# A graph layer's edge rows picked from three bfloat16 parts instead of float32 halves

## The chip, the core and the metric

The kernel runs on one core of one Trainium2 chip. Five engines of the core matter here: PE multiplies matrices (its weight loads are listed apart as PEld), DVE does elementwise work and reductions, ACT does copies and activation functions, POOL issues the indirect transfers that scatter rows, and SP issues most of the other transfers. Each engine works through its own instructions in the order of the program and stops at an instruction whose inputs aren't there. The metric is the device time of one execution in microseconds. Before the change it was 2373.37 us (median of 3 runs, 2369.18 to 2377.8).

## The reference

There are 12500 nodes with 64 features and 212500 edges (`src`, `dst`), sorted by `dst`, each with a weight. Each edge's input is put together from its two nodes and its weight and goes through two layers; the results are summed by `src`, and two more layers give the node's new features.

```python
h = jnp.maximum(_layernorm(x, axis=-1), 0.0)
edge_in = jnp.concatenate([h[src], h[dst], edge_weight1], axis=1)
e = silu(edge_in @ eW1 + eb1)
e = silu(e @ eW2 + eb2)
agg = segment_sum(e, src, num_segments=12500)
node_in = jnp.concatenate([h, agg], axis=1)
out = x + silu(node_in @ nW1 + nb1) @ nW2 + nb2
```

## The kernel before

The first layer is split by its inputs. For every node two rows of 128 numbers are worked out once: table `ta` (the part that comes from the `src` node) and table `tb` (from the `dst` node; `tb0` is a copy of the part that the first edges need). What an edge needs is then `ta[src] + tb[dst] + weight * eW1[last] + eb1`.

**Sending (`send_all`, `count`, `send`).** The edges are taken in 208 blocks of 1024, two blocks to a pair. As edges are sorted by `dst`, the 256 edges of a quarter of a block find all their `tb` rows in a window of 30 rows. `windows` loads the eight windows of a pair into one of three `win` buffers; a quarter's window lies on 32 partitions, on rows 30 and 31 of which stand `eW1[last]` and `eb1`. `load_rows` brings the edges' row numbers within their windows (`bc`, repeated on 32 partitions) and `count` compares them on DVE with the partition's number (L408, or L406 and L402 for the last and first pairs): `pick` has a one where an edge's row is. `weights` loads the edge weights into row 30 of each quarter of `pick`, and row 31 is one. `send` multiplies `pick` by `win` on PE in float32, on 64 partitions at a time (L475), which gives `tb[dst] + weight * eW1[last] + eb1` for 2 x 128 edges; ACT copies it to a buffer `qs` and writes the edge's place within its bucket beside it (L484, L485); POOL scatters 128 rows by one indirect transfer to the list `q` in DRAM (L488). The rows are sorted into 100 buckets of 125 `src` nodes: where a row goes is worked out in `count`, from how many of each bucket came before (L393 to L451), and is handed to POOL in the tile `to` (4 buffers). There are 16 buffers of `qs`, each with two tiles of 128 edges.

**Steps.** The rows of the buckets are read back in 18 levels of 25 batches, 450 steps in all (`s_lr` to `s_add`), each with 4 tiles of 128 edges: PE builds one-hot matrices, adds `ta[src]` (L596, L610, L616), ACT applies Silu (L620), PE the second layer (L648), ACT Silu again (L652), PE sums by node (L662), DVE adds to `aggT` (L673). The load of a batch (`fetch`, L559, on SP) waits until the scatters of all blocks of its level have landed. In the last level the node part (`nodes`) follows.

**Order.** The order of the instructions on PE, DVE, ACT and SP is written out by hand. Ahead of the steps stands the start: `first_rows` makes the four groups of `tb0`, `destinations` and `by_edges`, `sources` and `scale` turn the edge lists into bucket numbers, `products` makes 25 groups each of `ta` and `tb`, while the first blocks are already sent. A list of generators (`feed`) deals out the pieces of this between the pieces of `send_all`. Later, `marks` says how many pieces of sending are to stand before each step, and they are put between the stages of the steps. POOL's own order is that in which the scatters are written.

Of the kernel before, what the change touches and what calls it, by code (L numbers as in the profile page):

```python
# [42 lines left out]
SPAN = 7 * STEP + WL  # L43
# [21 lines left out]
FILL0, FILL_EACH, FILL_LATE = 18, 2, 8  # L65
AFTER = mybir.DependencyInfo(mybir.DependencyClass.Sync, mybir.DependencyReason.DATA)
# [8 lines left out]
def tile_gnn(ctx: ExitStack, tc: tile.TileContext, x, src, dst, ew, eW1, eb1, eW2, eb2, nW1, nb1, nW2, nb2, out):  # L75
# [105 lines left out]
    for g in range(2):  # L181
        nc.vector.tensor_scalar(
            same0[:, g : g + 1], plus, float(STEP), float(g * NQR * STEP), op0=OP.mult, op1=OP.add
        )
    nc.vector.tensor_scalar(plus, same, float(WL + 1), None, op0=OP.is_equal)
# [15 lines left out]
    tb = dram.tile([P * NB, H], F32, name="tb")  # L201
    dests = dram.tile([NP, NQR, 2, QR], BF16, name="dests")

    tb0 = dram.tile([FRONT + P * NE, H], F32, name="tb0")
    ta_buckets, tb_buckets = (t.rearrange("(l b) f -> l b f", b=NB) for t in (ta, tb))

    def product(s, hr, ps, tag, to):

        abs_ = []
        for a in range(2):  # L210

            half = slice(a * D, (a + 1) * D)
            ab = ps.tile([P, G // 2, H], F32, name="ab", tag=tag)
            for i in range(G // 2):
                nc.tensor.matmul(ab[:, i], hr[half, i, :], w1[half, s, :], start=True, stop=True)  # L215
            abs_.append(ab)
        for a in range(2):
            nc.scalar.copy(to.rearrange("l (i a) h -> l a i h", a=2)[:, a], abs_[a])
# [12 lines left out]
    wins = [const.tile([P, 2, 2, H], F32, name=f"win{i}") for i in range(NW)]  # L231
    nc.vector.memset(wins[0], 0.0)

    def extra_rows(dma, wins):

        for win in wins:
# [69 lines left out]
    qsp = ctx.enter_context(tc.tile_pool(name="qs", bufs=16))  # L306
    top = ctx.enter_context(tc.tile_pool(name="to", bufs=4))
    with ExitStack() as work:
# [17 lines left out]
        def load_rows(s):  # L326

            if s < nblocks:
                p, g = s // 2, s % 2
                if p == 0:  # L330
                    lists[p] = [None, None]
                    blk[s] = [None]
                    return
                if g == 0:
                    bc = ld.tile([P, 2, QR], BF16, name="bc")
                    lists[p] = [bc, None]
                    r = dests[p, 0, 0]
                    of = bass.AP(tensor=r.tensor, offset=r.offset, ap=[[2 * QR, NQR], [0, 32], [1, 2 * QR]])
                    nc.sync.dma_start(bc.rearrange("p g e -> p (g e)"), of)
                blk[s] = [lists[p][0][:, g]]  # L340

        def windows(p):

            table, front, end = (tb, FRONT, NB * P) if 2 * p >= EARLY else (tb0, 0, NE * P)
            if p == 0:
                table, end = tb0[: FRONT + G * P], G * P
            assert 2 * p < EARLY or len(done_b) == NB // G
            at = nc.sync.value_load(base_i[:, p : p + 1], min_val=front, max_val=FRONT + end - SPAN)
            for a in range(NQR):
# [3 lines left out]
                nc.sync.dma_start(wins[p % NW][a * 32 : a * 32 + WL, :, a % 2, :], of)  # L353

        def load(s):

            if s < nblocks:
                p, g = s // 2, s % 2
                if g == 0:
                    if p != 1:  # L360
                        windows(p)
                    lists[p][1] = ld.tile([P, 2, QR], F32, name="pick")
                blk[s] += [wins[p % NW][:, g], lists[p][1][:, g]]
            if s:
                load_rows(s + 1)

        def weights(s):

            if s < nblocks:
                p, g = s // 2, s % 2  # L370
                pick = lists[p][1][:, g]
                e0 = s * BLK
                m = 1 if e0 + 2 * BLK > E else 2
                if m == 2 or e0 + BLK <= E:
                    of = bass.AP(tensor=ew.tensor, offset=ew.offset + e0, ap=[[QR, NQR], [BLK, m], [1, QR]])
                    nc.sync.dma_start(lists[p][1][WL::32, g : g + m, :], of)
                else:
                    for a in range(NQR):
                        m = min(QR, E - e0 - a * QR)
                        if m > 0:  # L380
                            of = bass.AP(tensor=ew.tensor, offset=ew.offset + e0 + a * QR, ap=[[m, 1], [1, m]])
                            nc.sync.dma_start(pick[a * 32 + WL : a * 32 + WL + 1, :m], of)

        def count(s):

            if s < nblocks:
                bc, win, pick = blk[s]
                p, g = s // 2, s % 2
                whole = p > 0 and (2 * p + 2) * BLK <= E
# [15 lines left out]
                elif not whole:  # L405
                    nc.vector.tensor_scalar(pick, bc, same, plus, op0=OP.is_equal, op1=OP.add)  # L406
                elif g == 0:
                    nc.vector.tensor_scalar(lists[p][1], lists[p][0], same, plus, op0=OP.is_equal, op1=OP.add)  # L408
            yield
            if s < nblocks and p and (g == 0 or not whole):  # L410
                weights(s)
# [45 lines left out]
        def send(s):  # L457
# [6 lines left out]
            places = locE[:, g * TB : (g + 1) * TB, p].rearrange("p (i a t) -> p i t a", a=2, i=2)  # L464
            for t, i in itertools.product(range(2), range(2)):
                if i or t:
                    yield
                if i == 0:
# [9 lines left out]
                tiles = [j for j in (4 * i + t, 4 * i + 2 + t) if j < nt]  # L478
# [3 lines left out]
                qp = qps[i]  # L482
# [235 lines left out]
        def first_rows(g):  # L718

            hr = turned(x0, g)  # L720
            yield
            got = fp.tile([P, G, H], F32, name="got")
            product(1, hr, mm, "mm", got)
            yield
            nc.scalar.dma_start(tb0[FRONT + g * P : FRONT + (g + G) * P, :].rearrange("(p j) f -> p j f", j=G), got)
# [12 lines left out]
        def products(b0, g, xs):  # L738
# [15 lines left out]
            product(1, hr, mm, "mm", got)  # L754
            yield
            nc.sync.dma_start(tb_buckets[:, b : b + G, :], got)
# [15 lines left out]
        def destinations():  # L772
# [21 lines left out]
            for g in range(2):  # L794
                nc.vector.tensor_tensor(
                    rowsD[:, :, g, :],
# [98 lines left out]

        def checks():
# [24 lines left out]
        done_a, done_b, ready, scaled = [], [], set(), set()  # L921
# [12 lines left out]
        with tc.tile_pool(name="lists", bufs=1, side="right") as lp:  # L934
            x0 = lp.tile([P, NE, D], F32, name="x0")
            plus0 = lp.tile([P, 2, QR], F32, name="plus0")
            pair0 = lp.tile([2 * NQR, 2, P], F32, name="pair0")
# [12 lines left out]
            nc.sync.dma_start(tb0[:FRONT], zeros[:FRONT, :H])  # L950
            extra_rows(nc.sync.dma_start, wins[:1])
# [3 lines left out]
            f, sf = (lp.tile([NP, PAIR], F32, name=n) for n in ("f", "sf"))  # L955
# [6 lines left out]
            rowsD = lp.tile([NP, NQR, 2, QR], BF16, name="rowsD")  # L962
# [28 lines left out]
            list(table)  # L991
# [10 lines left out]
            list(counting)  # L1002
            todo = groups()
# [7 lines left out]
            for win in wins[1:]:  # L1011
                nc.vector.memset(win, 0.0)
            extra_rows(nc.sync.dma_start, wins[1:])
# [11 lines left out]
            lists_on = itertools.chain(*(g for part_ in parts for g in (sources(*part_), scale(*part_))), checks())  # L1025
# [96 lines left out]
def general_sums(tc, N, E, NB, H, src, dst, ew, ta, tb, aggT, w1d, eb1b, w2, ident, ones, eb2r, part):  # L1122
# [6 lines left out]
    with ExitStack() as ctx:  # L1129
# [17 lines left out]
        def tile_of(at, n):  # L1147
# [10 lines left out]
            for k, (idx, table) in enumerate(((si, ta[:]), (di, tb[:]))):  # L1158
                got = gw.tile([P, H], F32, name=f"got{k}")
# [6 lines left out]
                nc.vector.tensor_tensor(pre[:n], pre[:n], got[:n], op=OP.add)  # L1166
# [76 lines left out]
```

## Time and profile before

| | |
|---|---|
| median of 3 runs | 2373.37 us |
| profiled execution | 2374.24 us |
| its span | 2372.4 us |
| granted PE clock, mean | 0.962 |
| busy: PE, DVE, POOL, ACT | 89%, 78%, 72%, 50% |

The span goes from the first instruction of the profiled execution to its last. The page cuts it into 40 slices of 59 us and gives each engine's busy share in tenths. A group's row has the line, engine, operation, what it writes and reads, how often; then its busy time in us and the mean length of one in ns; then how long the engine stood idle just before instructions of the group, and which work ended most of that idle time. Names of tiles have their buffer numbers left out. POOL's indirect transfers are counted as busy while it writes their descriptors, not until the data have landed. Line numbers are those of the kernel before.

### The profile page before, as it was taken

The numbers are of one execution on the slowest core, as the hardware profiler recorded it, in microseconds if no ns is written. First come the engines' busy times: TensorE is split into PE (matmuls) and PEld (weight loads), VectorE is DVE, ScalarE is ACT, GpSimd is POOL, SyncE is SP. The second block draws the span as 40 slices with busy tenths as digits, with TensorE's granted clock in tenths as the row PEclk, the third lists the DMA queues.
The fourth block names the chain that finished last, engine by engine and source line by source line (L and its number), as shares of the span: only waits on it lengthen the run. The fifth ranks groups of instructions, "written<-read, shape, count | busy, mean of one in ns | idle before, by whom it ended". The sixth has DMA issues, their size and how long they took to land.

```text
span 2372.4 us, 49836 instructions
## 1 busy us (share of the span) xinstructions
PE 2103.3 (89%) x17399; PEld 1847.2 (78%) x17399; DVE 1857.0 (78%) x3291; ACT 1180.9 (50%) x3262; POOL 1697.3 (72%) x1711
## 2 busy tenths in 40 slices
PE   3685888789999999998999889999989999999998
PEld 2452667678888888887788778888878888889998
DVE  7985667678888888787888788878788888788665
ACT  3463554445555555554445445545455555555543
POOL 5677777777777777777777777777777777777310
PEclk9975899899999999999999999999999999999999
DMA  4475676555555555555555555555654444444564
GB/s 136 156 251 194 218 242 190 166 185 174 178 180 173 170 177 176 173 170 157 170 164 172 168 162 172 164 167 170 190 165 131 134 135 135 137 135 141 160 214 122
DMA packets 241429, 401.83 MB, mean 169 GB/s; under 512 B 47528, under 2 KB 140195, under 8 KB 240965
## 3 DMA queue, kind: packets, MB, share of 16 engines
q1 hardware_dynamic: 149411, 216.21, 30.7%
q0 software_dynamic: 53568, 123.20, 14.5%
q10 hardware_dynamic: 38192, 59.17, 8.8%
q8 instruction: 139, 2.28, 0.4%
q14 instruction: 119, 0.97, 0.1%
HBM read 191.09 MB, written 207.01 MB: 168 GB/s over the span
## 4 chain that ended last, share of the span: by engine, by line
PE 50%; DMA 22%; DVE 11%; POOL 6%; issue 6%; ACT 4%; DVEq 0%; SPq 0%; ACTq 0%; POOLq 0%
DMA q<-qs,to 16%; PE seg L662 11%; PE pt L616 10%; PE p L648 8%; POOL q L488 6%; PE qp L475 6%; DMA qt<-q 6%; PE pt L610 6%; PE lr L596 3%; DVE aggT L673 2%; DVE each L398 1%; PE ab L215 1%; ACT e L620 1%; PE z L286 1%; PE o L295 1%
## 5 line engine op out<-in xcount | busy, mean ns | idle before, releaser
L488 POOL DMA_INDIRECT q<-qs,to x1661 | 1669.2, 1005 | 542.5 <-issue 306.1
L620 ACT ACTIVATE e<-pt 128x512 f32<-128x512 f32 x450 | 268.9, 597 | 765.5 <-PE pt L616 704.3
L662 PE MATMUL seg<-one,e 128*128 128x125 f32 x3600 | 505.0, 284 | 106.1 <-DVE aggT L673 89.4
L662 PEld LDWEIGHTS seg<-one,e 128*128 128x128 f32 x3600 | 445.9, 195 | 144.3 <-DVE aggT L673 72.8
L648 PE MATMUL p<-w,e 128*128 128x128 f32 x3600 | 486.1, 278 | 0.0
L648 PEld LDWEIGHTS p<-w,e 128*128 128x128 f32 x3600 | 441.9, 192 | 12.5 <-issue 10.5
L484 ACT COPY qs<-qp 128x256 f32<-128x256 f32 x831 | 309.2, 372 | 266.6 <-PE qp L475 261.4
L601 DVE TENSOR_SCALAR oneT<-lr,part 125x512 f32<-125x512 f32 x450 | 335.1, 745 | 19.2 <-PE lr L596 12.8
L673 DVE TENSOR_TENSOR aggT<-aggT,seg 128x500 f32<-128x500 f32 x425 | 284.4, 669 | 64.6 <-PE seg L662 61.2
L475 PE MATMUL qp<-win,pick 64*128 64x256 f32 x1662 | 319.3, 452 | 17.0 <-ACT qs L484 5.9
L629 DVE TENSOR_TENSOR one<-nodes,qt 128x500 f32<-128x500 f32 x450 | 302.7, 673 | 0.0
L610 PE MATMUL pt<-ident,qt 128*128 128x128 f32 x1800 | 286.1, 283 | 1.4 <-ACT zn L267 0.9
L652 ACT ACTIVATE e<-p 128x512 f32<-128x512 f32 x450 | 269.6, 599 | 30.2 <-PE p L648 18.9
L642 ACT COPY p<-b2f 128x512 f32<-128x512 f32 x450 | 267.6, 595 | 0.0
L616 PE MATMUL pt<-oneT,al 125*128 125x128 f32 x1952 | 262.2, 278 | 0.0
L451 DVE SCALAR_TENSOR_TENSOR to<-rank,offE 128x8 int32<-128x8 f32 x208 | 36.6, 176 | 286.7 <-DMA q<-qs,to 282.1
L616 PEld LDWEIGHTS pt<-oneT,al 125*128 125x128 f32 x1952 | 242.2, 195 | 0.0
L447 DVE TENSOR_TENSOR mine<-oh,counts 128x800 f32<-128x800 bf16 x208 | 204.0, 981 | 39.8 <-PE counts L432 39.5
L596 PE MATMUL lr<-identb,qt 128*125 128x128 bf16 x1800 | 186.9, 228 | 49.6 <-DMA qt<-q 49.1
L610 PEld LDWEIGHTS pt<-ident,qt 128*128 128x128 f32 x1800 | 196.5, 145 | 27.2 <-issue 22.9
L596 PEld LDWEIGHTS <-qt 128*125 128x125 bf16 x1800 | 156.9, 141 | 76.3 <-DMA qt<-q 63.7
L449 DVE TENSOR_REDUCE rank<-mine 128x8 f32<-128x800 f32 x208 | 205.1, 986 | 7.2
(176 smaller groups left out, 1945.7 us busy)
## 6 DMA issues: line engine op xcount, KB each, us to landing
qt<-q SPq DMA_DIRECT2D x450, 288.0 KB
q<-zeros ACTq DMA_DIRECT2D x70, 720.0 KB
q<-qs,to POOLq DMA_INDIRECT x1661
bc<-dests SPq DMA_DIRECT2D x103, 128.0 KB
win<-tb SPq DMA_DIRECT2D x416, 30.0 KB
tb<-got SPq DMA_DIRECT2D x25, 256.0 KB
zd<-zn SPq DMA_DIRECT2D x25, 250.0 KB
zh<-zd SPq DMA_DIRECT2D x25, 250.0 KB
```

The source lines that it names most:

```text
L475: nc.tensor.matmul(qps[i_][:, :m], pick[half, t * P : (t + 1) * P], win[half, :m], start=True, stop=True)
L484: nc.scalar.copy(qs[:, :m, :H], qp[:, :m, :])
L488: ins = nc.gpsimd.indirect_dma_start(out=q[:], out_offset=bass.IndirectOffsetOnAxis(ap=to[:k, j : j + 1], axis=0), in_=qs[:k, a, :], in_of ...
L596: nc.tensor.matmul(lr[:L, t, :], loc[:, at : at + 1].to_broadcast([P, L]), identb, start=True, stop=True)
L601: nc.vector.tensor_scalar(oneT, st[k].pop("lr")[:L], part1[:L, :], None, op0=OP.is_equal)
L610: nc.tensor.matmul(pt[:, t, :], qt[:, j, :H], ident, is_transpose=True, start=t == 0, stop=False, skip_group_check=True)
L616: nc.tensor.matmul(pt[:, cols, :], a[:L, b, :], oneT[:, cols, :], start=False, stop=True, skip_group_check=True)
L620: nc.scalar.activation(e1, pt, AF.Silu)
L629: nc.vector.tensor_tensor(one.rearrange("p (b j) l -> p b j l", j=n), nodes1[:, None, None, :].to_broadcast(wide), loc[:, tiles[0][1] : ti ...
L648: nc.tensor.matmul(p2[:, t, :], e1[:, t, :], w2, start=False, stop=t == G - 1, skip_group_check=True)
L662: nc.tensor.matmul(item[2][:, b, :], e2[:, t, :], one[:, t, :], start=j < G, stop=j >= G * (n - 1))
L673: nc.vector.tensor_tensor(v, v, seg, op=OP.add)
```

## The change

The rows of `tb` are kept as three bfloat16 parts, which together hold the float32 value, side by side in DRAM. A window then takes 32 rows of three parts each, that is 96 partitions, and 12 more partitions take `eW1[last]` and `eb1` in their parts against the parts of the edge weights and ones: 108 partitions (`K3`) in all. All eight windows of a pair are brought by one load, the row numbers of all 2048 edges by one (`picks`, repeated on 96 partitions) and the weights' parts by one. The compare is done in place on 96 x 2048 bfloat16, once for a pair. `send` has one bfloat16 product of 108 partitions for every 128 edges, where one float32 product on 64 partitions served 256 edges. The first pair is still done in float32, from a table `tbF` of its own.

What must be worked out for this: `product` splits each group of `tb` into three parts (two copies, two subtractions, one copy, one subtraction, through `got3`, which has one buffer), `split` does the same to the first group, `first_weights` to the weights of the first pairs and to the two extra rows, and `other_weights` to the rest of the weights, in eight pieces, dealt out at the head of the lists. The edge lists are turned to float32 in place, and `qs` has 10 buffers instead of 16, for room.

```diff
+WT = 32
+SPAN = 7 * STEP + WT
+K3 = 3 * WT + 12
...
+    def split(parts, of, rest_):
+        with nc.allow_low_precision("three parts hold every bit"):
+            nc.scalar.copy(parts[0], of)
+            nc.vector.tensor_tensor(rest_, of, parts[0], op=OP.subtract)
+            nc.scalar.copy(parts[1], rest_)
+            nc.vector.tensor_tensor(parts[2], rest_, parts[1], op=OP.subtract)
...
+        if parts is not None:
+            v = parts.rearrange("l (i a) c h -> l a i c h", a=2)
+            with nc.allow_low_precision("three parts hold every bit"):
+                for a in range(2):
+                    nc.scalar.copy(v[:, a, :, 0], abs_[a])
+                    nc.vector.tensor_tensor(to[:, a], abs_[a], v[:, a, :, 0], op=OP.subtract)
+                nc.scalar.copy(v[:, :, :, 1], to)
+                nc.vector.tensor_tensor(v[:, :, :, 2], to, v[:, :, :, 1], op=OP.subtract)
+            return
...
-    qsp = ctx.enter_context(tc.tile_pool(name="qs", bufs=16))
+    qsp = ctx.enter_context(tc.tile_pool(name="qs", bufs=10))
...
-                    bc = ld.tile([P, 2, QR], BF16, name="bc")
-                    of = bass.AP(tensor=r.tensor, offset=r.offset, ap=[[2 * QR, NQR], [0, 32], [1, 2 * QR]])
-                    nc.sync.dma_start(bc.rearrange("p g e -> p (g e)"), of)
+                    of = bass.AP(tensor=r.tensor, offset=r.offset, ap=[[0, 3 * WT], [1, PAIR]])
+                    nc.sync.dma_start(picks[p % NW][: 3 * WT], of)
+                    of = bass.AP(tensor=w.tensor, offset=w.offset, ap=[[NP * PAIR, 4], [0, 3], [1, PAIR]])
+                    nc.sync.dma_start(picks[p % NW][3 * WT : K3], of)
...
+            if p:
+                rows = table[bass.ds(at - front, SPAN), :]
+                of = [[H, 3 * WT], [STEP * 3 * H, 2 * NQR], [1, H]]
+                of = bass.AP(tensor=rows.tensor, offset=rows.offset, ap=of)
+                nc.sync.dma_start(wins[p % NW][: 3 * WT], of)
+                return
...
-                    nc.vector.tensor_scalar(lists[p][1], lists[p][0], same, plus, op0=OP.is_equal, op1=OP.add)
+                    both = picks[p % NW][: 3 * WT]
+                    nc.vector.tensor_scalar(both, both, same3[: 3 * WT], None, op0=OP.is_equal)
...
+                if p:
+                    i, t = t, i
+                    qp = mm.tile([P, 2, H], F32, name="qp", tag="mm")
+                    for a, j in enumerate(range(4 * i + 2 * t, min(4 * i + 2 * t + 2, nt))):
+                        nc.tensor.matmul(
+                            qp[:, a], pick[:K3, j * P : (j + 1) * P], win[:K3, 2 * i + t], start=True, stop=True
+                        )
...
+            got3 = fp.tile([P, G, 3, H], BF16, name="got3", bufs=1)
+            product(1, hr, mm, "mm", got.rearrange("l (a i) h -> l a i h", a=2), got3)
+            yield
+            nc.sync.dma_start(tb_buckets[:, b : b + G, :], got3.rearrange("l j c h -> l j (c h)"))
...
+        def other_weights():
+            lists_in(sf, ew, nc.sync.dma_start)
+            wR = sf
+            m = PAIR // 8
+            w4s = [lp.tile([NP, 4, m], BF16, name=f"w4{i}") for i in range(2)]
+            yield
+            for w4 in w4s:
+                nc.vector.memset(w4[:, 3].bitcast(F32), TWO_ONES)
+            for c in range(8):
+                v, w4 = wR[:, c * m : (c + 1) * m], w4s[c % 2]
+                with nc.allow_low_precision("three parts hold every bit"):
+                    nc.scalar.copy(w4[:, 0], v)
+                    yield
+                    nc.vector.tensor_tensor(v, v, w4[:, 0], op=OP.subtract)
+                    nc.scalar.copy(w4[:, 1], v)
+                    yield
+                    nc.vector.tensor_tensor(w4[:, 2], v, w4[:, 1], op=OP.subtract)
+                to = weighs[0, FIRST * PAIR + c * m :]
+                to = bass.AP(tensor=to.tensor, offset=to.offset, ap=[[PAIR, NP - FIRST], [NP * PAIR, 4], [1, m]])
+                nc.sync.dma_start(to, w4[FIRST:])
+                yield
+            weighed.update(range(FIRST, NP))
...
-            lists_on = itertools.chain(*(g for part_ in parts for g in (sources(*part_), scale(*part_))), checks())
+            lists_on = itertools.chain(other_weights(), *(g for part_ in parts for g in (sources(*part_), scale(*part_))), checks())
```

In the order of the program, block 0's split, the first weights and two rows to be split stand ahead of ACT's first copy to `qs`. Counting pairs of tiles copied to `qs` (four to a block), the 25 groups of `tb` stand between pairs 13 and 72, where they stood between 13 and 61.

More of the change, by code (lines that the diff above doesn't have):

```diff
@@ L1010, in tile_gnn @@
             next(sending)
[L1011 to L1013 removed]
+            list(weighing)
             lists_in(srcR, src, nc.scalar.dma_start)
```

141 lines of the change are left out of this document (87 added, 54 removed).

## The prediction

> **What bounds the kernel now.** I read the page's busy shares first, then the groups by line, then asked who POOL, the engine that issues the scatters of edge rows (L488), waited for.
>
> ```profile
> span 2372.4 us, 49836 instructions
> ...
> PE 2103.3 (89%) x17399; PEld 1847.2 (78%) x17399; DVE 1857.0 (78%) x3291; ACT 1180.9 (50%) x3262; POOL 1697.3 (72%) x1711
> ...
> POOL 5677777777777777777777777777777777777310
> ...
> L488 POOL DMA_INDIRECT q<-qs,to x1661 | 1669.2, 1005 | 542.5 <-issue 306.1
> ```
>
> By busy share PE looks like the bound (89%) and POOL like an engine with room (72%). But POOL's row is flat from the third slice to the fourth from the end. The waits of POOL alone between 102 and 2203 us, and its timeline where that stretch ends, say why:
>
> ```profile
> POOL q L488 <- issue: 295.8, 971, 0.3
> POOL q L488 <- DMA q<-qs,to: 76.2, 250, 0.3
> ```
> ```profile
> 2204.62 0.96 POOL L488 DMA_INDIRECT q<-qs,to  x1 [2.18 <-ACT qs L485]
> 2221.28 0.96 POOL L488 DMA_INDIRECT q<-qs,to  x1 [0.31 <-issue]
> ```
>
> The last column of the waits is the longest one, and it is 0.3 us for every releaser: a fixed step between two scatters, put down to whatever ended nearby. So for 2100 us POOL never waits for data. One scatter costs 1.005 + 0.30 = 1.305 us, and 1661 of them are 2168 us of the 2372. POOL's queue is the bound; PE, in program order, keeps step with it: DVE, which feeds POOL its row numbers, stands still until earlier scatters land and their buffers come free.
>
> ```profile
> DVE to L451 <- DMA q<-qs,to: 282.1, 123, 6.8
> ```
>
> After the last scatter at 2221 PE works off what is left. In the chain of waits a landed scatter is the last thing that isn't PE's, and from 2127 on PE leads:
>
> ```profile
> 2123.43 2.28 DMA q<-qs,to
> 2126.94 1.16 PE seg L662 x8
> ```
>
> The profiled run took 2374.24 us (1.8 us of it outside the span), 0.9 above the median of 2373.37; I count from 2374.2. About 0.3% (7 us) is what a measurement here can tell from no change.
>
> **Part 1, products: one bfloat16 product per tile.** It takes time from PE. Between 2124 and 2223 us, the one stretch with such products in which PE leads, they are busy for 8.4 us of 99:
>
> ```profile
> 2124.00:2223.00 99.00, 8.42 (x46) 3.61 (x46) 1.00 0.44 135
> ...
> L475 PE MATMUL qp<-win,pick 64*128 64x256 f32 x1662 | 319.3, 452 | 17.0 <-ACT qs L484 5.9
> L596 PE MATMUL lr<-identb,qt 128*125 128x128 bf16 x1800 | 186.9, 228 | 49.6 <-DMA qt<-q 49.1
> ```
>
> A bfloat16 product of this size adds 186.9/1800 = 0.104 us of busy time, so eight per block cost 0.83 us where a block now costs 319.3/208 = 1.53. Over 208 blocks that frees some 145 us of PE, but only where PE leads does it count: 8.4 x (1 - 0.83/1.53) = 3.8, and I take **-3**. Everywhere else the freed time becomes PE waiting for POOL.
>
> **Part 2, the picks on DVE, and what they do to POOL.** One compare per pair on 96 x 2048 bfloat16, in place, replaces one on 128 x 512 that wrote float32. The nearest rows, and what such an instruction does to a scatter that begins under it:
>
> ```profile
> L408 DVE TENSOR_SCALAR pick<-bc,same,plus 128x512 f32<-128x512 bf16 x102 | 55.6, 545 | 0.0
> L406 DVE TENSOR_SCALAR pick<-bc,same,plus 128x256 f32<-128x256 bf16 x2 | 0.8, 404 | 0.0
> L860 DVE TENSOR_SCALAR locE<-locE 128x384 f32<-128x384 f32 x4 | 1.5, 367 | 0.1
> L860 DVE TENSOR_SCALAR locE<-locE 128x128 f32<-128x128 f32 x1 | 0.2, 228 | 0.0
> L629 DVE TENSOR_TENSOR one<-nodes,qt 128x500 f32<-128x500 f32 x450 | 302.7, 673 | 0.0
> L290 DVE TENSOR_TENSOR zs<-z,zh 128x250 f32<-128x250 f32 x50 | 19.6, 417 | 4.8 <-PE z L286 1.1 <-DMA out_dram<-os 0.8 <-issue 0.5
> ```
> ```profile
> 1507.19 0.98 DVE L449 TENSOR_REDUCE rank<-mine 128x8 f32<-128x800 f32 x1
> 1507.83 0.96 POOL L488 DMA_INDIRECT q<-qs,to  x1 [0.30 <-issue]
> ...
> 1508.89 0.56 DVE L393 TENSOR_TENSOR oh<-numbers,bkB 128x800 bf16<-128x800 bf16 x1
> 1509.10 1.20 POOL L488 DMA_INDIRECT q<-qs,to  x1 [0.30 <-DVE one L629]
> ...
> 1510.40 0.54 DVE L408 TENSOR_SCALAR pick<-bc,same,plus 128x512 f32<-128x512 bf16 x1
> 1510.60 1.17 POOL L488 DMA_INDIRECT q<-qs,to  x1 [0.30 <-issue]
> ```
>
> The scatter under the reduction takes its 0.96 us. The one that began 0.20 us into the pick takes 1.17: it ran on by 0.21 after losing what was left of the pick less some 0.12. So a pick holds POOL up for its remainder. A pick of d us meets an issue with chance d/1.305 and costs half of d on average: 0.545 x 0.545 / 2.61 = 0.11 us, 12 us over 102 picks. The new d: the two picks' rows give 0.55 ns a column and 0.26 fixed, the two L860 rows 0.54 ns and 0.16. At that rate 2048 columns take 1.39 us and hold POOL for 0.74 us a pick, +64 in all; at half of it, as all operands are two bytes wide, 0.70 to 0.82, say 0.76 us, 0.22 us a pick, 23 us in all. Lower end: one column at a time with POOL left alone as under the reduction, -12. I take 0.76, **+11** (23 - 12), since every one-input compare here runs at two columns of four-byte output and this writes half as many bytes.
>
> The Trainium skill, VectorE: DVE Perf Modes, "The perf-mode tier table", has such a compare at 693 ns for 2048 bfloat16 columns; by that the term would be 0.18 x 102 - 12 = +7, an estimate from that page. Its page Advanced Engine Details and Errata, "VectorE Performance Modes", says that two-port Vector instructions and GpSimd block each other, which speaks against this change; the stretched scatter at 1510.60 agrees.
>
> **Part 3, windows, lists and weights on the queues.** Per pair SP issues 3 loads in place of 6 (4 windows, one list, one weight row). The list grows from 128 to 384 KB and the windows come in runs of 256 bytes in place of 512. They go out over a block ahead, as the list does now, and PE has slack there: **0**; if the cover were gone a pair would wait for one landing, 1.86 us for today's windows (row below), 1.86 x 103 = 192 at the very worst. Against a gain stands that POOL has no wait to lose.
>
> **Part 4, the ring of qs shrinks from 16 to 10 buffers.** ACT now stops when the tenth pair before has not landed, where DVE stopped (L451) twelve to sixteen pairs behind. POOL keeps 10 x 2 x 1.305 = 26 us of work ahead, against L451's longest wait of 6.8, so it isn't starved. But PE arrives at the PE-led end two pairs later behind POOL: 2 x 2.61 = **+5** (0 to 10).
>
> **Part 5, the start.** Four places, all ahead of 235 us, where POOL has little queued, and their rows:
>
> ```profile
> 19.77 0.17 DVE L451 SCALAR_TENSOR_TENSOR to<-rank,offE 128x8 int32<-128x8 f32 x1
> ...
> 20.80 1.06 POOL L488 DMA_INDIRECT q<-qs,to  x1 [10.29 <-DVE base L791]
> ```
> ```profile
> 37.88 0.65 ACT L218 COPY got<-ab 128x256 f32<-128x256 f32 x2 [1.31 <-PE ab L215]
> ...
> 41.04 0.65 ACT L218 COPY got<-ab 128x256 f32<-128x256 f32 x2 [1.31 <-PE ab L215]
> ```
> ```profile
> L642 ACT COPY p<-b2f 128x512 f32<-128x512 f32 x450 | 267.6, 595 | 0.0
> ```
> ```profile
> 41.72 2.27 DMA tb<-got
> 44.80 1.86 DMA win<-tb
> 46.90 1.90 PE qp L475 x4
> ```
> ```profile
> 51.00:105.00 54.00, 29.80 (x145) 19.68 (x143) 50.92 (x102) 18.76 (x67) 32.03 (x32) 1.00 0.38 129
> 105.00:235.00 130.00, 84.81 (x532) 57.76 (x530) 89.65 (x160) 65.69 (x242) 99.74 (x100) 0.72 0.66 221
> ```
> ```profile
> 6.42 0.81 SPq L974 DMA_DIRECT2D dstR<-in_dst_dram  x2
> ...
> 14.90 1.90 ACT L785 CAST f<-dstR 104x2048 f32<-104x2048 int32 x1 [3.26 <-DMA dstR<-in_dst_dram]
> ```
>
> The columns of the two long rows are the stretch, its length, PE, PEld, DVE, ACT and POOL. (a) ACT splits block 0's rows, the first weights and two rows ahead of the first copy to qs: after the row numbers at 19.94, DVE 0.67, ACT 0.60 (L642's 595 ns), DVE 0.67, then five short steps of some 0.3, so the first scatter comes 3.7 us later. POOL's one new memset lies in the 10.29 us that it waits there. (b) The second pair waits for three more groups of tb0. Each now takes copy 0.65, subtract 0.42, copy 0.60, subtract 0.67, issue 0.35 and a write of 2.27, one after another because got3 has one buffer: 5.0 us in place of the 3.2 between today's copies. The products at 46.90 move to about 55. With (a) in it: **+8** (4 to 12). (c) The remaining weights are read (768 KB, as the lists) over srcR while ACT has their copy queued ahead of qs: **+3** (0 to 8: a list of this size lands 8 us after its issue below). (d) From 51 to 105 DVE is busy 50.9 of 54 us and POOL issues 32 scatters where 54 us hold 41. Into this go 16 subtractions of weights (0.42 each, 6.7) and the splits of the five groups there (2 x 0.42 + 0.67 = 1.5 each, 7.5): **+14** (0 if they fall later). (e) From 105 to 235 some twenty groups add 30 us to DVE, which has 40 idle; ACT and DVE hand each group to and fro twice: **+4** (0 to 25). Their last subtractions (two SBUF inputs, like L393's above; length by L629) hold POOL up as picks do, 0.67 x 0.67 / 2.61 = 0.17 us each: **+3** with the weights' (0 to 5).
>
> Sum: -3 + 11 + 0 + 5 + 8 + 3 + 14 + 4 + 3 = +45, so 2374.2 + 45 = **2419 us**.
>
> **The rivals.**
> *PE bounds it after all* (faster). For: 89% busy, and between 2127 and 2221 PE leads. Against: POOL's longest wait is 0.3 us over 2100 us. If POOL were merely kept busy by PE's pace, 145 us less PE work would come off, 2230; with the start charged, 2262. It decides from the point where POOL's gaps between 102 and 2203 exceed 0.30 us; none does. 0.05. A milder kind: the pick leaves POOL alone (-12) and the start is hidden, 2374 - 12 - 3 + 5 = 2364. 0.04.
> *The start is hidden.* POOL's queue fills again by 105 us, so (c) to (e) would cost nothing: 2374 - 3 + 11 + 5 + 4 = 2391, and with the short pick and no shift at the end 2378. For: DVE has 40 us idle later. Against: idle time that comes later does not give POOL back an empty slot. 0.15, of which 0.06 is within 0.3%.
> *The pick runs at two columns* (1.39 us): 2419 - 11 + 64 = 2472. No row here has a one-input compare at four. 0.10.
> *The groups go in a convoy.* One got3 buffer and two hand-overs make each group take its 5.0 us and some 3 of waits, against the 6.8 us that POOL gives it (21 groups over 55 pairs): 21 x 1.2 = 25 more, with (e) at its end (21 above what I took) 2419 + 21 + 25 = 2465. 0.16.
>
> **How the numbers follow.** My forecast, 2395 to 2443 (startup terms at half to one and a half), has 0.50. Below 2378 lie the two faster cases, 0.09; above 2475 the worst of the last two, some 0.08. So 2378 to 2475. Faster 0.09; within 0.3% 0.06; slower 0.85.
>
> **What would show it.** Right: POOL's waits in the long stretch stay at 0.3; its first scatter near 24.5; larger gaps in POOL before 235 than now; the last scatter some 40 us later than 2221; PE's share lower, ACT waiting for landed scatters ahead of the copy to qs in place of DVE at L451; the pick at 0.70 to 0.82 us, scatters that begin under it stretched to its end; about 150 us from the last scatter to the end. Wrong: a mean scatter below 1.0 us or POOL with gaps in mid-run (PE or the ring bounds), a pick of 1.4 us, or a last scatter at 2225.

## The result, and the profile after

The changed kernel takes 2442.89 us (median of 4 runs, 2440.09 to 2444.89) against 2374.04 us for the kernel before (4 runs): a ratio of 1.029, 95% interval 1.0268 to 1.0313. It is slower, by 69 us where 45 were predicted. The profiled execution took 2440.09 us. From its page, the lines that answer to those of before:

```profile
span 2438.3 us, 49143 instructions
...
PE 1982.9 (81%) x17398; PEld 1869.5 (77%) x17398; DVE 1927.6 (79%) x3399; ACT 1202.2 (49%) x3312; POOL 1729.2 (71%) x1712
...
POOL 4755677777777777777777777777777777777410
...
L514 POOL DMA_INDIRECT q<-qs,to x1661 | 1701.2, 1024 | 575.5 <-issue 327.7
L510 ACT COPY qs<-qp 128x256 f32<-128x256 f32 x831 | 310.3, 374 | 804.2 <-DMA q<-qs,to 636.6
```

PE lost 120 us of work (2103.3 to 1982.9) and the kernel gained nothing by it. The products' own row fell from 319.3 us to 239.2:

```profile
L489 PE MATMUL qp<-win,pick 108*128 108x128 bf16 x1645 | 239.2, 231 | 78.8 <-ACT qs L510 52.6
```

POOL's row is as flat as before, but it gets there later: its second to fifth slices are 7, 5, 5, 6 where they were 6, 7, 7, 7. POOL's waits between 300 and 2260 us, the commonest and the longest, and its timeline at its first and its last scatter:

```profile
POOL q L514 <- issue: 290.3, 953, 0.3
...
POOL q L514 <- ACT qs L510: 13.0, 42, 0.5
```
```profile
25.43 1.06 POOL L514 DMA_INDIRECT q<-qs,to  x1 [15.02 <-ACT qs L511]
...
2285.80 1.27 POOL L514 DMA_INDIRECT q<-qs,to  x1 [0.30 <-issue]
```

From the last scatter's start to the end it is 152.5 us, where it was 151.1. So all but 1.4 us of the loss lies ahead of that scatter, and POOL's queue still sets the time. Where it fell behind shows when scatters are counted by stretch. The rows give the stretch, its length, and POOL's busy time in scatters with their count. First the kernel before:

```profile
20.00:100.00 80.00, 47.16 (x46) 1.00 0.41 136
100.00:300.00 200.00, 153.39 (x154) 0.77 0.67 222
300.00:2290.00 1990.00, 1468.63 (x1463) 0.98 0.54 167
```

and the changed one:

```profile
20.00:100.00 80.00, 46.01 (x44) 1.00 0.63 188
100.00:300.00 200.00, 124.40 (x121) 0.91 0.59 192
300.00:2290.00 1990.00, 1530.80 (x1498) 0.95 0.61 184
```

At 100 us it is two scatters behind, at 300 us 35. At 1.31 us each, those 35 are 46 us of the 64.5 by which the last scatter starts later. The other 18.5 come after 300 us: a scatter takes 1530.80/1498 = 1.022 us there, before 1468.63/1463 = 1.004. Summed from POOL's timeline, its gaps above 0.30 us come to 39.6 us between 100 and 300 us, where they were 0.7; up to 100 us they are 15.7 and were 18.5.

Those longer scatters can be put down to DVE instructions. Here and below, a scatter's excess is its time over 0.957 us, the length of an undisturbed one, and it goes to the DVE instruction whose end fits the scatter's end best. From 300 us on:

| us of excess under | before | changed |
|---|---|---|
| the pick (L408; L426) | 10.5 (59 scatters) | 24.4 (91) |
| `one`, the one-hot compare (L629; L655) | 41.8 (148) | 53.4 (165) |
| `oh` (L393; L412) | 12.2 (64) | 12.7 (61) |
| all | 68.8 | 97.0 |

That is 28 us more, of which 8 are given back: the scatters of before had some gaps over 0.30 us after 300 us that are gone. Two pairs of rows from the timeline of the changed kernel at 1500 us, a DVE instruction and the scatter that begins under it:

```profile
1505.11 0.67 DVE L655 TENSOR_TENSOR one<-nodes,qt 128x500 f32<-128x500 f32 x1
1505.24 1.37 POOL L514 DMA_INDIRECT q<-qs,to  x1 [0.30 <-issue]
...
1510.57 0.74 DVE L426 TENSOR_SCALAR pick<-pick,same 96x2048 bf16<-96x2048 bf16 x1
1510.77 1.37 POOL L514 DMA_INDIRECT q<-qs,to  x1 [0.30 <-issue]
```

The second scatter begins 0.20 us into the pick. 0.54 us of the pick are left, and the scatter runs 0.41 over: what is left less 0.13, as in the trace before.

What held the start back is in the waits of all engines between 100 and 300 us:

```profile
PEld ab L234 <- ACT hr L741: 63.1, 18, 7.9
...
ACT got L242 <- DVE got L241: 31.1, 21, 5.6
...
POOL q L514 <- ACT qs L511: 20.7, 11, 5.7
DVE got L241 <- ACT got L240: 20.5, 12, 3.6
PE qp L489 <- DVE got L241: 18.2, 6, 5.9
ACT var L727 <- DVE var L726: 15.1, 7, 5.3
ACT xs L722 <- DVE cen L718: 14.4, 6, 5.2
```

Three of these were there in the kernel before, and shorter:

```profile
PEld ab L215 <- ACT hr L715: 15.5, 13, 2.7
...
ACT var L701 <- DVE var L700: 4.7, 5, 2.7
...
ACT xs L696 <- DVE cen L692: 3.2, 2, 2.1
```

So ACT waits for DVE in the new splits (31.1 us), and 21.6 us longer than before in work that the change doesn't touch (`var` and `xs`); PE then waits for ACT's copy `hr`, the input of a table's next products. One place of the first kind, from the timeline:

```profile
184.56 2.28 DVE L981 TENSOR_REDUCE ends<-dstR 104x8 f32<-104x2048 f32 x1
...
187.15 0.75 DVE L241 TENSOR_TENSOR got<-ab,got 128x256 f32<-128x256 f32 x2
187.62 0.37 PE L489 MATMUL qp<-win,pick 108*128 108x128 bf16 x2 [5.21 <-DVE got L241]
...
187.93 0.62 ACT L242 CAST got<-got 128x512 bf16<-128x512 f32 x1 [5.60 <-DVE got L241]
...
190.50 0.35 ACT L510 COPY qs<-qp 128x256 f32<-128x256 f32 x1
...
191.24 0.96 POOL L514 DMA_INDIRECT q<-qs,to  x1 [4.51 <-ACT hr L741]
```

DVE comes late to the subtraction L241, as a reduction of 2.28 us is ahead of it. ACT stands 5.60 us at L242, the group's second copy, and the copies to `qs` are behind it. PE stands 5.21 us at its next products, because `ab` and `qp` share the same four PSUM buffers and those of `ab` now come free only when DVE has subtracted. POOL runs dry for 4.51 us.

### The profile page after: what moved, and what is told of

Same layout as the page of the kernel before. It is cut to its first block, busy times and chain, and to the rows that moved or that the text cites. A ratio compares the mean times of both kernels' runs of the same rounds, so it can differ in the third digit from the quotient of the medians.

```text
span 2438.3 us, 49143 instructions
## 1 busy us (share of the span) xinstructions
PE 1982.9 (81%) x17398; PEld 1869.5 (77%) x17398; DVE 1927.6 (79%) x3399; ACT 1202.2 (49%) x3312; POOL 1729.2 (71%) x1712
## 3 DMA queue, kind: packets, MB, share of 16 engines
q8 instruction: 139, 2.28, 0.4%
## 4 chain that ended last, share of the span: by engine, by line
DMA 32%; PE 25%; POOL 11%; DVE 11%; issue 9%; ACT 6%; ACTq 0%; POOLq 0%; DVEq 0%; SPq 0%
DMA q<-qs,to 30%; POOL q L514 11%; PE pt L642 6%; PE p L674 6%; PE seg L688 5%; PE pt L636 3%; ACT qs L510 2%; DMA qt<-q 2%; PE lr L622 1%; DVE oneT L627 1%; ACT e L646 1%; DVE mine L463 1%; DVE aggT L699 1%; DVE one L655 1%; PE qp L489 1%
## 5 line engine op out<-in xcount | busy, mean ns | idle before, releaser
L514 POOL DMA_INDIRECT q<-qs,to x1661 | 1701.2, 1024 | 575.5 <-issue 327.7
L674 PE MATMUL p<-w,e 128*128 128x128 f32 x3600 | 513.8, 288 | 17.5 <-ACT p L668 17.5
L688 PE MATMUL seg<-one,e 128*128 128x125 f32 x3600 | 500.4, 283 | 12.2 <-DVE aggT L699 10.9
L674 PEld LDWEIGHTS p<-w,e 128*128 128x128 f32 x3600 | 465.6, 201 | 24.1 <-ACT p L668 20.3
L688 PEld LDWEIGHTS seg<-one,e 128*128 128x128 f32 x3600 | 450.9, 197 | 16.8 <-ACT qs L511 5.8
L636 PE MATMUL pt<-ident,qt 128*128 128x128 f32 x1800 | 292.3, 287 | 83.7 <-ACT qs L510 77.1
L627 DVE TENSOR_SCALAR oneT<-lr,part 125x512 f32<-125x512 f32 x450 | 334.9, 744 | 25.3 <-PE lr L622 25.1
L489 PE MATMUL qp<-win,pick 108*128 108x128 bf16 x1645 | 239.2, 231 | 78.8 <-ACT qs L510 52.6
L655 DVE TENSOR_TENSOR one<-nodes,qt 128x500 f32<-128x500 f32 x450 | 301.5, 670 | 0.0
L642 PE MATMUL pt<-oneT,al 125*128 125x128 f32 x1936 | 269.3, 284 | 0.0
L489 PEld LDWEIGHTS <-pick 108*128 108x128 bf16 x1645 | 161.0, 105 | 116.7 <-issue 106.2
L642 PEld LDWEIGHTS pt<-oneT,al 125*128 125x128 f32 x1936 | 248.7, 201 | 0.0
L463 DVE TENSOR_TENSOR mine<-oh,counts 128x800 f32<-128x800 bf16 x208 | 204.0, 981 | 43.6 <-PE counts L448 43.6
```

Source lines behind the costliest of these rows:

```text
L489: nc.tensor.matmul(qp[:, a], pick[:K3, j * P : (j + 1) * P], win[:K3, 2 * i + t], start=True, stop=True)
L514: ins = nc.gpsimd.indirect_dma_start(out=q[:], out_offset=bass.IndirectOffsetOnAxis(ap=to[:k, j : j + 1], axis=0), in_=qs[:k, a, :], in_of ...
L627: nc.vector.tensor_scalar(oneT, st[k].pop("lr")[:L], part1[:L, :], None, op0=OP.is_equal)
L636: nc.tensor.matmul(pt[:, t, :], qt[:, j, :H], ident, is_transpose=True, start=t == 0, stop=False, skip_group_check=True)
L642: nc.tensor.matmul(pt[:, cols, :], a[:L, b, :], oneT[:, cols, :], start=False, stop=True, skip_group_check=True)
L655: nc.vector.tensor_tensor(one.rearrange("p (b j) l -> p b j l", j=n), nodes1[:, None, None, :].to_broadcast(wide), loc[:, tiles[0][1] : ti ...
```

## The experiments

The theory: POOL's queue sets the time, and the change costs what keeps POOL from issuing, first in the start, then by longer scatters. The rivals: PE, or the loads, set the time; or the loss lies in the ring of `qs`, the splits or the picks alone.

Each run is compared with runs of the kernel before on its own chip. Chips differ more than expected. On the chip of `b_qs10b`, `a_nosplitb` and `a_pick2b` the kernel before takes 2371.07 us; on those of all the other runs it takes 2904 to 2961 us, and there something else sets the time (last experiment). Both kinds are given with their ratios; times of different chips are not compared.

**The splits left out.** Each group of `tb` is copied three times by ACT. There are no subtractions, and nothing is handed between ACT and DVE. ACT copies half as much again (six copies of 256 columns a group, where the split has two of 256 and one of 512), and two of the three parts are wrong.

```diff
-                    nc.scalar.copy(v[:, a, :, 0], abs_[a])
-                    nc.vector.tensor_tensor(to[:, a], abs_[a], v[:, a, :, 0], op=OP.subtract)
-                nc.scalar.copy(v[:, :, :, 1], to)
-                nc.vector.tensor_tensor(v[:, :, :, 2], to, v[:, :, :, 1], op=OP.subtract)
+                    for c in range(3):
+                        nc.scalar.copy(v[:, a, :, c], abs_[a])
```

> The kernel after with each group of tb copied three times by ACT instead of split, once more where the kernel before takes 2374 us. If the start is lost in the splits: 2405 to 2420, POOL's gaps above 0.30 us near 40 us in place of 69.5. If the time goes in mid-run: 2438 to 2443. The output is wrong as before, for the second and third parts are copies of the first.

Measured: 2399.14 us, ratio 1.0118 (1.0089 to 1.0147), 28 us above the kernel before on the same chip, where the changed kernel was 69 above on its own: some 41 us of the loss are gone. That is 6 us below the range expected if the start is lost in the splits. In its profiled execution (2386.49 us, the fastest of five) the count of scatters up to 300 us is that of the kernel before again (47 and 154, before 46 and 154), though the longer splits of the first group and of the weights are still in it:

```profile
20.00:100.00 80.00, 48.40 (x47) 1.00 0.71 213
100.00:300.00 200.00, 153.03 (x154) 0.95 0.74 240
300.00:2290.00 1990.00, 1484.87 (x1462) 0.95 0.62 184
```

So the splits of these 28 groups (25 of `tb` and three of `tb0`) are the whole loss of the start, and what is lost there stays lost. The run takes away DVE's work and the handing over together; it doesn't part the two. From 300 us on the excess is 86.1 us here, of it 25.1 under the pick.

**One got3 buffer, or the handing over.** Is it the one buffer, as in the convoy rival, or the chain within a group?

```diff
-            got3 = fp.tile([P, G, 3, H], BF16, name="got3", bufs=1)
+            got3 = fp.tile([P, G, 3, H], BF16, name="got3", bufs=2)
...
-    qsp = ctx.enter_context(tc.tile_pool(name="qs", bufs=10))
+    qsp = ctx.enter_context(tc.tile_pool(name="qs", bufs=8))
```

> The changed kernel with two got3 buffers in place of one (room for it is made by 8 buffers of qs in place of 10, which by the 6.6 us that six fewer cost the kernel before is worth about +2). If the one got3 buffer puts the groups of tb in a convoy (one group's split waiting for the last one's write of 2.3 us), the start is shorter: 2415 to 2435. If it is the work of the splits itself and the two hand-overs between ACT and DVE in each group that hold the sending up, the second buffer gives nothing: 2441 to 2450.

Measured: 2883.37 us, ratio 0.9902 (0.9873 to 0.9932), on a chip where the expected times don't apply. But the start can be read there, by the scatters issued between 100 and 300 us, against two kernels on such chips. With one buffer (the doubled products below), with two, and with the splits left out (the first run of that kernel, further below):

```profile
100.00:300.00 200.00, 112.08 (x108) 0.88 0.51 168
```
```profile
100.00:300.00 200.00, 118.39 (x115) 0.50 0.55 181
```
```profile
100.00:300.00 200.00, 125.99 (x126) 0.50 0.58 191
```

Two more kernels with one buffer issue 111 in that stretch (a_psum on the same chip, a_pick2 on the chip of the third). So the second buffer gives back 4 to 7 of 15 to 18 scatters. This agrees with the changed kernel's own waits: ACT stands at L240 for a landed `tb<-got` for 8.3 us in all, and at L242 for DVE for 31.1. The one buffer is the smaller part. The larger is the rest of the split: DVE's work and the handing over.

**The ring alone.** The kernel before with 10 buffers of `qs` instead of 16.

```diff
-    qsp = ctx.enter_context(tc.tile_pool(name="qs", bufs=16))
+    qsp = ctx.enter_context(tc.tile_pool(name="qs", bufs=10))
```

> The kernel before with 10 buffers of qs, once more where the kernel before takes 2374 us. POOL's queue as the bound: 2374 to 2384. The ring as the cost: 2420 to 2443.

Measured: 2377.65 us (10 runs), ratio 1.0028 (1.001 to 1.0045), that is +6.6 us. The wait moves from DVE's `to` (282.1 us, now 81.0) to ACT:

```profile
ACT qs L484 <- DMA q<-qs,to: 615.5, 396, 6.7
...
DVE to L451 <- DMA q<-qs,to: 81.0, 56, 4.0
```

The price is near the predicted +5, but not by the predicted way. From the last scatter's start (2226.66) to the end it is 151.5 us, as before (151.1). The last scatter itself starts 5.4 us later, and the excess from 300 us on is 73.3 instead of 68.8. It may be the rhythm of DVE against POOL; but two profiles of one kernel below differ by 4 us in their scatters as well (1613.7 and 1609.9), so that this isn't shown.

**The compare done twice.** The changed kernel with a second compare behind the pick, in place, that leaves it as it is.

```diff
                     nc.vector.tensor_scalar(both, both, same3[: 3 * WT], None, op0=OP.is_equal)
+                    nc.vector.tensor_scalar(both, both, 1.0, None, op0=OP.is_equal)
```

> The kernel after with the second compare behind each pick, once more, to be read where the kernel before takes its 2374 us (on the other chip it took 2961 and POOL had gaps all along). There POOL has none, so the theory that an instruction of this kind holds POOL up says +0.2 to 0.23 us a pair over the 2443 of after: 2463 to 2467, or 2505 if POOL can't get in between the two compares; DVE's time alone, with DVE waiting for landed scatters, says 2443.

Measured: 2442.32 us, ratio 1.0296 (1.0266 to 1.0325): no cost at all, against 2463 to 2467 by the theory: a miss. The two compares in that trace:

```profile
L426 DVE TENSOR_SCALAR pick<-pick,same 96x2048 bf16<-96x2048 bf16 x103 | 77.1, 749 | 0.0
L427 DVE TENSOR_SCALAR pick<-pick 96x2048 bf16<-96x2048 bf16 x103 | 71.1, 690 | 3.5
```

The second one meets 39 scatters for 6.7 us, the pick 91 for 25.4. The scatter of 1510.77 shown above, held up by the pick until 1511.31, runs on for 0.83 us, and the next begins 0.30 us later. By then the 0.69 us of a second compare are over. So two compares back to back don't hold POOL up twice as long: the expectation took each as meeting scatters at random. That account of the miss is read from the traces; no run tests it. The remaining 7 us are not seen in the time either: up to 300 us four scatters fewer are issued than in the changed kernel (161 against 165), but the excess under `one` is 43.6 us in this profile where it was 53.4. The Trainium skill, VectorE: DVE Perf Modes, "The perf-mode tier table", gives 693 ns for this size; the second compare, against a constant, agrees (690), and the pick, against a number per partition, takes some 60 ns more.

**The excess taken away.** Does the second SBUF input of `one` hold POOL up, as the table above supposes? The node numbers are put in PSUM, beside the counts (for a tile of their own, `b_psum`, PSUM had no room, so that run gave no result):

```diff
-        full = sgp.tile([P, NB], F32, name="counts")
+        both_ = sgp.tile([P, NB + L], F32, name="counts")
+        full, nodesP = both_[:, :NB], both_[:, NB:]
...
+        nc.vector.tensor_copy(nodesP, nodes1)
...
-                nodes1[:, None, None, :].to_broadcast(wide),
+                nodesP[:, None, None, :].to_broadcast(wide),
```

In the kernel before:

> The kernel before, with the node numbers that the one-hot compare (one, L629) reads moved from SBUF to PSUM, beside the counts; nothing else is changed, and the numbers are the same. Between 300 and 2200 us of the trace of before, scatters that begin under L629 are longer than the 0.957 us floor by 38.4 us in all, those that begin under additions with one PSUM input by next to nothing. POOL's queue is the bound: L629 stops stretching scatters, POOL's busy time falls by about 38 us, partly made up for by other lines that then catch more of them, so 2328 to 2350 us. Rival (PE, or the loads, are the bound and POOL only keeps pace): the freed time turns into gaps of POOL and the time stays at 2366 to 2382.

and in the changed kernel:

> The changed kernel with the same edit (the node numbers that L655 reads lie in PSUM). There scatters that begin under L655 are stretched by 51.8 us in all between 300 and 2200 us. POOL's queue as the bound: 2392 to 2418 us, some 25 to 50 below the changed kernel's 2443, and PE's share up. Rival (another engine or the loads set the pace): 2436 to 2450.

The expectations' 38.4 and 51.8 count by the instruction under way at the scatter's start alone; by the rule above they are 41.8 and 53.4. Both ran on a chip where the kernel before takes 2914.09 us. The scatters' rows, of b_psum2 and of a_psum:

```profile
L490 POOL DMA_INDIRECT q<-qs,to x1661 | 1613.7, 972 | 1160.4 <-ACT qs L487 430.1
```
```profile
L516 POOL DMA_INDIRECT q<-qs,to x1661 | 1625.3, 979 | 1119.2 <-ACT qs L513 491.7
```

and the timeline of a_psum at a scatter that begins 0.14 us into the compare:

```profile
1508.19 0.67 DVE L657 TENSOR_TENSOR one<-counts,qt 128x500 f32<-128x500 f32 x1
1508.33 0.96 POOL L516 DMA_INDIRECT q<-qs,to  x1 [2.38 <-ACT qs L513]
```

On such chips the scatters take 1660.8 us in the kernel before with ten buffers, and 1680.7 in the changed kernel with doubled products (a_qp2b), in which `one` reads both inputs from SBUF. So the edit takes off 47 and 55 us; between 300 and 2300 us the excess under `one` falls from some 34 us in both to 0.0 and 0.8. That the second SBUF input is the cause is shown. The Trainium skill, GPSIMD Engine Reference, "8. Key points", says so of instructions with two SBUF inputs as of two-port ones, and both agree here.

The times say nothing of what it is worth: 2940.39 us, ratio 1.0089 (1.0056 to 1.0122), and 2906.15 us, ratio 0.9969 (0.9947 to 0.9991). POOL has long waits for ACT's copies there (the last column of its row), so shorter scatters free nothing. And the compare now shares a tile with the counts, so that PE waits for it: `counts` at L415 and L434 stand 59.0 and 61.8 us for `one`, which they never did. Both times miss the ranges expected with POOL's queue as the bound, as it isn't the bound there. The kernel before was run so once more:

> Once more the kernel before with the node numbers that its one-hot compare (one) reads in PSUM in place of SBUF. On the chip where the kernel before takes 2914 us this took 47 us off POOL's scatters (1661 to 1614 us) and nothing off the time, as POOL wasn't the bound there. On a chip where the kernel before takes about 2373 us and POOL's gaps are 0.30 us: if POOL's queue is the bound, 2325 to 2350 us. If another engine is close behind POOL (PE is at 89%, and the compare now shares a tile with the counts that PE writes, so the two wait for each other), part of it comes back as gaps of POOL, 2350 to 2366; if POOL only kept pace, 2366 to 2400.

Measured: 2944.74 us, ratio 1.0142 (1.0093 to 1.019), once more where the kernel before takes 2904. What the edit gives where POOL's queue sets the time stays open.

**Twice the products, and the chips on which POOL isn't the bound.** The doubled products, and three of the edits above under labels of their own (a_pick2, a_nosplit, b_qs10), ran on a chip where the kernel before takes 2960.99 us; the doubled products also where it takes 2914.09.

```diff
-                        nc.tensor.matmul(
+                        for _ in range(2):
+                            nc.tensor.matmul(
```

> The kernel after with every bfloat16 product of the picks done twice into the same place: some 0.104 us x 1645 = 171 us more of PE's time, about what the change took from it. If PE bounds anything but the end, +100 to +170: 2540 to 2610. If POOL's queue bounds the run, only the products after PE takes the lead count, about 50 x 0.104 = 5 us: 2443 to 2451, with PE near 88% busy.

> The kernel after, with a second compare (equal to one, in place, same 96 x 2048) behind each pick; the values stay as they are. DVE has room (79% busy), so if only DVE's time counted nothing would change: 2443. If an instruction of this kind holds POOL up for its remainder, 0.2 to 0.23 us a pair as the pick does, 103 pairs: 2463 to 2467, with the mean scatter 13 ns longer; if POOL can't get in between the two compares, about 0.64 us a pair, 2505.

> The kernel after with each group of tb copied three times by ACT instead of split: no subtractions on DVE and no hand-overs between ACT and DVE for the 28 groups, as many bytes copied on ACT and written; the second and third parts are wrong and so is the output. If the start is lost in these splits, POOL's gaps above 0.30 us fall from 69.5 us in all towards the 36.6 of before: 2405 to 2420. If the start were hidden and the time went in mid-run: 2438 to 2443.

> The kernel before with 10 buffers of qs instead of 16 and nothing else. If POOL's queue bounds the run and the ring only moves PE two pairs closer behind it, 2374 to 2384 us, POOL's gaps in mid-run at 0.30 us, and ACT instead of DVE waiting for landed scatters. If the shorter ring itself is what costs (ACT waits 637 us for landed scatters after the change), most of the 69 us: 2420 to 2443.

> The changed kernel with every bfloat16 product of send done twice, the second over the first's result with the same value; 1648 more products of 0.104 us, some 170 us of PE. POOL's queue as the bound: PE has that room nearly everywhere, only the stretch at the end in which PE leads grows by some 5 us: 2443 to 2452. Rival (PE is the bound): the 170 us come on top wherever PE leads, 2540 to 2610.

| run | us | ratio to before | interval |
|---|---|---|---|
| b_qs10 | 2957.98 | 0.9998 | 0.9975 to 1.002 |
| a_pick2 | 2929.28 | 0.9891 | 0.9859 to 0.9924 |
| a_qp2 | 2943.8 | 0.9939 | 0.9909 to 0.9968 |
| a_nosplit | 2904.53 | 0.9794 | 0.9755 to 0.9832 |
| a_qp2b (2914.09) | 2895.32 | 0.9922 | 0.9892 to 0.9951 |

None of the expected times applies, and the sign has turned: versions of the changed kernel are 0.3 to 1.1% faster than the kernel before, without the splits 2%. The changed kernel itself didn't run there. From the page of b_qs10:

```profile
PE 54%; issue 13%; another core or an unknown queue 11%; POOL 7%; DVE 6%; ACT 5%; DMA 3%; SPq 0%; ACTq 0%; POOLq 0%; DVEq 0%
...
L488 POOL DMA_INDIRECT q<-qs,to x1661 | 1660.8, 1000 | 1129.0 <-ACT qs L485 444.9
```

POOL stands idle for 1129 us, mostly behind ACT's copies. DVE's and ACT's instructions take the same as ever (the reduction at L449 986 ns, the copy at L484 375 against 372), but PE's take longer: for the same kernel PE is busy for 2367.8 us here and 2144.3 in `b_qs10b`, and the mean granted PE clock is 0.884 here and 0.964 there. 24% of the chain are pauses put to "issue" or to an unknown queue. What makes these chips slower wasn't tried; the lower clock is one candidate, but PE's 223 us more are less than half of the 573 us between the two spans.

That these versions win here because PE has less work is likely, but not shown. The doubled products add 96 us to PE's busy time (2170.1 in a_pick2, 2266.4 in a_qp2), where the expectation took 171, and the time is 14.5 us longer; as these two differ in the second compare as well, the price of doubling alone isn't known. That doubled products cost nothing where POOL's queue is the bound wasn't measured either. For that chip the evidence against PE is that POOL's waits stay at 0.3 us, and that without the splits the kernel is still 28 us slower with 121 us less of PE's work (1982.2 us busy, against 2103.3 in the trace before).

## Why the prediction was right, and where it was wrong

The direction, the bound and the range were right; 2419 was 24 us low, and 2442.89 lies at the very end of the forecast's 2395 to 2443, about as near to the convoy rival's 2465. Step by step, in the profiled executions:

| step | predicted, us | measured, us |
|---|---|---|
| 1 products, at the end, and 4 ring | -3 and +5 | +1.4 from the last scatter to the end; ring alone +6.6 ahead of it, not counted here as it is within the rows below |
| 2 picks | +11 | +14 (24.4 less 10.5) |
| 3 windows, lists | 0 | 0: PE's waits for windows are 1.1 us in all |
| 5 start, (a) to (e) and the subtractions | +32 | +46 (35 scatters) |
| not foreseen: excess under `one` and `oh` | 0 | +12 (53.4 + 12.7 less 41.8 + 12.2) |
| gaps of POOL after 300 us (see the products) | 0 | -8 |

The measured column comes to 65.4 of the 65.9 us between the two spans.

- *The bound* holds: POOL's longest wait in the long stretch is 0.5 us, once. The two cases in which PE bounds or the start is hidden fell.
- *The products* are mis-sized: one takes 239.2/1645 = 0.145 us of PE, where 0.104 was taken from the row of L596, so less of PE came free than reckoned. The 3 us were to be gained between 2124 and 2223 us. In the trace before POOL has five gaps there, from 2204 to 2220, 8.2 us above the usual 0.30; the changed kernel has none at its end, the ring alone 10.0 us, and the two other runs with the new products on that chip 2 and 6 us. So a gain at the end may be theirs; neither that nor its size is shown.
- *The picks* came out by their own working. The pick takes 756 ns where 0.76 us was taken; it costs 24.4/103 = 0.24 us of POOL each where 0.22 was worked out.
- *The start* is the term that was mis-sized, and its parts stood in the wrong places. (a) and (b) are about right (first scatter at 25.43 instead of 24.5; the second pair's copy to `qs` at 58.40 where it was 48.12, 10 us later). (c) is seen as a wait of 4.2 us of ACT for the weights. But by 100 us all of it, with the 14 us of (d), has been made up for: POOL is two scatters behind, and these are some 3 us, where (a) to (d) were to cost 25. The step that failed is (e), "DVE, which has 40 idle; ACT and DVE hand each group to and fro twice: +4". With the subtractions, for which 3 us were taken, it cost 33 scatters, 43 us. That 32 us in all came as near to 46 as they did is luck: two errors of opposite sign. DVE's idle time was taken as room, but what counts is when DVE gets to a subtraction: ACT, in program order, holds the copies to `qs` behind it, and PE its next products for want of a PSUM buffer. That PE waits for DVE too was overlooked.
- *The convoy* rival had nearly that size (50 us for (e) and its convoy) but named the one got3 buffer and the two hand-overs together as its cause. The second buffer gave 4 to 7 of 15 to 18 scatters back, so the buffer is the smaller part.
- *The ring* came near the size predicted by luck: at the end of the kernel, where it was charged, 0.4 us of it show.
- *The excess under `one`* went from 41.8 to 53.4 us without any change to it; it was 49.2 with ten buffers of `qs` and 47.2 with the splits left out. Some of it may be the rhythm of 10 buffers. This is not settled.

## What to carry to other kernels

Ask first which queue sets the time, then charge a change by what it takes from that queue: 120 us less of PE's work gave nothing, the splits in the start 43 us. When an engine in program order hands work to another and waits for it back, ask what stands behind the waiting instruction and which buffer is held meanwhile; the busy time and the mean idle share of either engine didn't show that cost here. A count of the bottleneck's instructions by stretch of time shows at once where it fell behind.

## What was not expected of the hardware

- Chips differ: the kernel before takes 2371 us on one and 2904, 2914 and 2961 us on three others, with equal durations of DVE's and ACT's instructions, a lower granted PE clock (0.884 against 0.964 for one kernel) and longer pauses. A change that is 2.9% slower on the one is 0.3 to 1.1% faster on the others (in the variants run there), where POOL stands idle for 1129 us and so no longer sets the time.
- A second compare of 0.69 us right behind one of 0.75 us held POOL up for 6.7 us in all, the first for 25.4.
- A two-input compare held up scatters when both inputs were in SBUF (some 34 us under `one` between 300 and 2300 us) and no longer when one was in PSUM (0.0 and 0.8).
